# A two-layer mixture-of-experts kernel: sums of x in one piece, branch hints one instruction block ahead, layer 0's branch behind its fourth pair

## Chip, cores, metric

The kernel runs on one core of one Trainium2 chip. The metric is the time of one execution on the device in microseconds (us); less is better. Its engines are TensorE (PE, matrix products), VectorE (DVE), ScalarE (ACT), GpSimd (POOL) and SyncE (SP, which here issues most of the DMAs and does no arithmetic). Each engine works through its own list of instructions in order; semaphores make one wait for another.

## What is computed

Sixteen batches of 256 rows by 256 columns go through two residual layers. Which weights a batch meets depends on its row of `cond_8`.

```python
expert = jnp.argmax(opcode_onehot, axis=-1)                     # layer 0: one of 8 experts
up   = einsum('bsd,bhd->bsh', x, W_up[expert]) + b_up[expert]
gate = einsum('bsd,bhd->bsh', x, W_gate[expert]) + b_gate[expert]
x = x + einsum('bsh,bdh->bsd', silu(up) * gate, W_down[expert]) + b_down[expert]

rw = softmax(cond); w, sel = top_k(rw, 2); w = w / w.sum()      # layer 1: two of 8 experts
mlp(x, g, u, d) = (gelu(x @ g) * (x @ u)) @ d
x = x + sum_k w_k * mlp(x, expert sel_k) + mlp(x, shared)
```

The hidden width is 512 in layer 0 and 1024 in layer 1. All is float32.

## The kernel before

**Units.** Two batches that use the same expert make a Pair; a batch left over is a Single. A Pair's products are done with seven matrix products of half-size blocks where eight would be needed by the plain rule: `STEPS` lists them, with the blocks of the weights (A11, S2, ...) and of x (B11, T2, ...). The blocks named S and T are sums and differences, and have to be made first:

- of x: `sums_x` (L455) with `sums_b` (L467 to L473), three DVE operations, one of 512 columns (L470) and two of 256 (L471, L472). They write `bt` (layer 0) or `xt` (layer 1), and in layer 0 the second writes a `dz` buffer.
- of the up and gate weights of one quarter: `sums_q` (L483), four POOL operations (L478 to L481), or for the shared expert a DMA of sums kept in DRAM.
- of the down weights: `sums_d` (L500), the same four on larger blocks.
- of the activations, before the down product: `act_sums` (L584), again `sums_b`.

**Quarters.** A Pair's hidden width is cut in `kp` parts, two in layer 0 and four in layer 1, each called a quarter here. `up(j, k)` (L536) issues product k of quarter j into a PSUM bank: X, Y and Q, two banks each. After product 0, 2 and 4 ACT copies X out (`copy`, L525); DVE adds or subtracts that copy and Y or Q into `c` (`combine`, L529), which is what lets the bank be used again. `act` (L569) has ACT apply gelu (L573) or silu (L580) and DVE multiply by the gate (L574, L581). `down(k)` (L589) issues the down products into banks A, B (one each) and Y; `early` reads bank A (in layer 1 on ACT, L621; in layer 0 on DVE, L616), and `late` writes the result `ys` (L628, L632).

**Order.** Everything is written out by hand by `Line` (L820). It keeps a clock in which each of the first six products of a quarter counts 2. `main` issues a product, moves the clock and then issues whatever `later` has due. Instructions due at the same time go in the order of their due times. So the order on every engine follows from the due times: product 6 of a quarter is due 4 after its other products, its `act` 6, its `act_sums` 12, the down products 18 and on after the Pair's last quarter.

When a quarter begins, `quarter` (L879) calls `ahead` (L845), which issues the loads: q (up and gate weights) five quarters ahead, sums_q and x three ahead, the sums of x one ahead (L862 to L865), and the quarter's own down weights d. `when_free` puts a step off until a buffer is given back. `quarter` then sends results of earlier units, and runs `route` (L910): the sorting of batches by expert for layer 1 is recorded as a list of small DVE steps, and one to a few are issued per quarter.

**The work and its two branches.** How many Pairs and Singles there are depends on the data. Layer 0 always has batch 0 alone (`l0_first`), one more Single and four Pairs (`l0_pairs`); its remainder is zero to three Pairs and Singles. Layer 1 has eight Pairs on the shared expert (`shared`), twelve Pairs for certain (`pairs`), and zero to four more. A program is written out for each count, and every engine jumps to the one it needs with a table branch: `arms(0)` after `units[0]`, and inside each arm `arms(1)`. In this run both remainders are three Pairs. The register that chooses is loaded in `announce` (L893), which also gives each engine a hint of where its branch (line L1077) will lead. Before the change `units[0]` are the first two Pairs of layer 0, `tails[0]` the other two, and all five engines are hinted at the same point: when the last-but-one quarter of the last unit before the branch begins (L887 to L889). Behind the first branch come the two Pairs of `tails[0]`, then the first five shared Pairs with layer 0's remainder between them, then layer 1's Pairs.

Of the kernel before, what the change touches and what calls it, by code (L numbers as in the profile page):

```python
# [11 lines left out]
ALU = mybir.AluOpType  # L12
# [8 lines left out]
NPR = B // 2  # L21
NA = 2 * B

NP1 = (B - 1 - E + 1) // 2
NP2 = (NA - E) // 2
NS1, NS2 = B - 1 - 2 * NP1, NA - 2 * NP2
NF = 5
NB = 3
# [23 lines left out]
C11, C21, C12, C22 = range(4)  # L52
# [7 lines left out]
def kernel(  # L60
# [8 lines left out]
    out: bass.AP,  # L69
):  # L70
    nc = tc.nc
    SP, POOL = mybir.EngineType.SP, mybir.EngineType.Pool
    ENGINES = [SP, POOL, *(getattr(mybir.EngineType, e) for e in ("PE", "DVE", "Activation"))]
    ctx.enter_context(tc.manual_schedule())

    const = ctx.enter_context(tc.tile_pool(name="const", bufs=1))
# [98 lines left out]
    made = {}  # L175
    steps = [[]]

    class Recorder:
# [5 lines left out]
        @staticmethod  # L184
        def step():
            steps.append([])
# [27 lines left out]
    def order_of_work(v, n, at, layer):  # L214

        tt, red = v.tensor_tensor, v.tensor_reduce
        a, b = square(0, n), square(1, n)  # L220
        numn = num[:, :n]

        def rows(t):
            return t.unsqueeze(2).to_broadcast([P, n, n])

        def cols(t):
            return t.unsqueeze(1).to_broadcast([P, n, n])

        def small(name, dt=F32):
            return const.tile([P, n], dt, name=f"{name}_{layer}")  # L230

        count, rank, odd, key, pos = map(small, ("count", "rank", "odd", "key", "pos"))
        ri = small("ri", I32)
        tt(b, rows(numn), cols(numn), ALU.is_gt)
        step(v)
        tt(a, rows(at), cols(at), ALU.is_equal)
        step(v)
        red(count, a, AX.X, ALU.add)
        step(v)
        tt(a, a, b, ALU.mult)  # L240
        step(v)
        red(rank, a, AX.X, ALU.add)
        step(v)

        v.tensor_copy(ri, rank)
        v.tensor_single_scalar(ri, ri, 1, ALU.bitwise_and)
        v.tensor_copy(odd, ri)
        tt(count, count, rank, ALU.subtract)
        tt(count, count, odd, ALU.add)
        v.tensor_scalar(count, count, 1.0, 4096.0, ALU.is_equal, ALU.mult)  # L250
        v.scalar_tensor_tensor(key, at, float(n), numn, ALU.mult, ALU.add)
        tt(key, key, count, ALU.add)
        tt(a, rows(key), cols(key), ALU.is_gt)
        step(v)
        red(pos, a, AX.X, ALU.add)
        step(v)
        tt(a, rows(numn), cols(pos), ALU.is_equal)
        step(v)

        def sorted_(dst, x):  # L260
            tt(b, a, x, ALU.mult)
            step(v)
            red(dst, b, AX.X, ALU.add)
            step(v)

        t = small("t")
        sorted_(t, cols(at))
        as_index(v, exs[layer], t, E, E - 1)
        made[layer, "e"] = len(steps)
        i = num[:, :B].unsqueeze(1).unsqueeze(1).to_broadcast([P, n, n // B, B])  # L270
        a4, b4 = (q.rearrange("p s (k b) -> p s k b", b=B) for q in (a, b))
        tt(b4, a4, i, ALU.mult)
        step(v)
        red(t, b, AX.X, ALU.add)
        step(v)
        as_index(v, bs[layer], t, 0, B - 1)
        made[layer, "b"] = len(steps)

        red(more, count, AX.X, ALU.add)
        step(v)  # L280
        v.tensor_scalar(more, more, -1.0 / (2 * 4096), E / 2, ALU.mult, ALU.add)
        v.tensor_scalar(more_i[layer], more, 0.0, float(MOST[layer]), ALU.max, ALU.min)
        if layer:
            sorted_(wsort, cols(wts.rearrange("p k b -> p (k b)")))
            v.tensor_scalar(nwsort, wsort, -1.0, None, ALU.mult)
# [7 lines left out]
    more = const.tile([P, 1], F32, name="more")  # L293
    MOST = ((NS1 - 1) // 2, NS2 // 2)
    more_i = [const.tile([P, 1], I32, name=f"more_{i}") for i in range(2)]
# [154 lines left out]
    class Pair(Unit):  # L450
        width, last = 2, False
        first, step = 18, None


        def sums_x(self, spread):  # L455

            self.x = {n: self.xt[:, i, :] for n, i in B_AT.items()}
            if not self.layer:
                self.x["T2"] = take("dz", S, of=(self, "T2"))
            for i, f in enumerate(self.sums_b(self.xt, self.x["T2"])):  # L460
                if spread:
                    line.later(2 + 4 * i, f)
                else:
                    f()

        @staticmethod
        def sums_b(t, t2):  # L467
            tt = nc.vector.tensor_tensor
            return (
                lambda: tt(t[:, 4:6, :], t[:, 0:3:2, :], t[:, 2:4, :], ALU.subtract),  # L470
                lambda: tt(t2, t[:, C22, :], t[:, 4, :], ALU.add),  # L471
                lambda: tt(t[:, 6, :], t[:, C21, :], t2, ALU.subtract),  # L472
            )  # L473

        @staticmethod
        def sums_a(a, s):
# [35 lines left out]
        def load_z(self):  # L512

            self.z = take("z", KD, 2, S)
            self.stores = [], []
            self.out = [self.row(out, t, e) for t, e in enumerate((SP, mybir.EngineType.Activation))]
            for t in range(2):
                nc.sync.dma_start(self.z[:, :, t, :], self.row(out, t))

# [63 lines left out]

        def act_sums(self, j):  # L584
            t = self.acts[j]
            for f in self.sums_b(t, t[:, 2, :]):
                f()

        def down(self, k):  # L589

# [189 lines left out]
    l0_first = First(next(names), 0, B - 1)  # L780
    l0_one = Single(next(names), 0, B - 2)
    l0_pairs = [Pair(next(names), 0, 2 * i) for i in range(NP1)]
    l0_more = [Pair(next(names), 0, 2 * NP1 + 2 * i) for i in range(MOST[0])]
    l0_ones = [Single(next(names), 0, 2 * NP1 + i) for i in range(NS1 - 1)]
    l0_one.po_bank = "A"
    shared = [Pair(next(names), 1, None, (2 * i, 2 * i + 1)) for i in range(NPR)]
    pairs = [Pair(next(names), 1, 2 * i) for i in range(NP2)]
# [2 lines left out]
    shared[-1].last = True  # L790
    shared[-2].step = 7

    units = [l0_pairs[: NP1 - 2], [*pairs, *shared[NF : NPR - NB]]]
    tails = [l0_pairs[NP1 - 2 :], shared[-NB : 1 - NB]]

    among = {
        u: [[] for _ in range(u.kp)] for u in [*l0_pairs, *l0_more, *pairs, *more_pairs, *shared]
# [22 lines left out]
    class Line:  # L820
# [24 lines left out]
        def ahead(self, i):  # L845

            at = dict(enumerate(quarters))
            if i + Q_AHEAD in at:
                u, j = at[i + Q_AHEAD]
                u.load_q(j)  # L850
            if i + S_AHEAD in at:
                u, j = at[i + S_AHEAD]
                if u.width == 2:
                    when_free("s", lambda u=u, j=j: u.sums_q(j))
                if j == 0:
                    if u.width == 2 and not u.layer:
                        when_free("bt", u.load_x)
                    else:
                        if u.layer:
                            self.send(0)  # L860
                        u.load_x()
            if i + 1 in at:  # L862
                u, j = at[i + 1]
                if u.width == 2 and j == 0:
                    u.sums_x(i > 1 and at[i][0].width == 2)  # L865
            if i < 0:
                return
            u, j = at[i]
            pair0 = u.width == 2 and not u.layer
            if j == pair0 and u is not l0_first:  # L870
                when_free(u.d_from, u.load_d)
            if pair0 and j:
                self.later(12, u.sums_d)
            elif u.width == 2 and j == 2:
                u.sums_d()
            if u is shared[-1] and j == 2:
                u.load_z()

        def quarter(self, unit, j):  # L879

            self.at += 1
            assert quarters[self.at] == (unit, j)
            self.ahead(self.at)
            self.send()
            for layer in range(2):

                u = units[layer][-1]  # L887
                if (unit, j) == (u, u.kp - 2):
                    self.announce(layer)  # L889
            for _ in range(self.routes(unit, j)):  # L890
                self.route()

        def announce(self, layer):  # L893

            n = MOST[layer] + 1
            self.arm = nc.values_load(
                more_i[layer][0:1, 0:1],
                min_val=0,
                max_val=n - 1,
                skip_runtime_bounds_check_because="held between 0 and the largest",  # L900
            )
            self.hint = tc.switch_hint(dict.fromkeys(ENGINES, self.arm), n)

        def routes(self, unit, j):

# [18 lines left out]
    line = Line()  # L924
# [63 lines left out]
    run(units[0])  # L988
    for k in arms(0):

        mid, further = [*tails[0]], l0_more[:k]
        for i, u in enumerate(shared[:NF]):
            mid.append(u)
            if i < len(further):
# [2 lines left out]
        places = [a for u in mid for a in among[u]]  # L997
        for a in places:
            a.clear()
        pieces = [p for u in l0_ones[2 * k :] for p in (u.ups, u.downs)]  # L1000
        for a, p in zip(places[3:], pieces):
            a.append(p)
        follow([*mid, *units[1], *tails[1]], behind=False)
        run([*mid, *units[1]])
# [77 lines left out]
```

## Time and profile before

| | us |
|---|---|
| time, three runs: median (lowest, highest) | 1071.49 (1070.37, 1071.58) |
| the profiled execution: its time | 1071.98 |
| the profiled execution: its span | 1070.3 |
| TensorE busy | 1043.4 |
| VectorE busy | 784.6 |
| GpSimd busy | 449.7 |
| ScalarE busy | 353.2 |

A span runs from the first instruction of the program to the last; the 1.7 us between span and time lie around it. A matmul's end is modelled, so a busy PE need not be PE at its best, but with one start each 216 ns (the median) the 4750 matmuls alone come to 1026 us. Rows of the profile name the engine, the line of the kernel, the operation, and what it writes and reads (`c<-cp,Q`). In the view of waits a row says who waited for whom: total us, how many times, the longest. In a listing by time a row has start and length in us, and in brackets how long the engine was idle before it and what ended that. "issue" is a wait for nothing that the profile shows, such as the instructions themselves.

### The profile page before, as it was taken

To read this page: it belongs to the slowest core of one execution; us is meant where nothing else is said; L and a number is where in the kernel's file an instruction comes from. 1 tells how busy PE (TensorE), PEld (TensorE's weight loads), DVE (VectorE), ACT (ScalarE), POOL (GpSimd) and SP (SyncE) were. 2 spreads that over 40 slices of the span, in tenths; PEclk is the share of its full clock that TensorE was granted. 3 is DMA by queue.
4 is the path that set the end of the run, shared out by engine and by line. 5 is a ranking of instruction groups with operands and counts; after the bars stand their busy time and mean duration, and the time that the engine had idled before them with its cause. 6 is when DMAs were issued, how large, how long until landed. Compare 5 with 4: busy or idle time off the path is not lost.

```text
span 1070.3 us, 14116 instructions
## 1 busy us (share of the span) xinstructions
PE 1043.4 (97%) x4750; PEld 899.6 (84%) x4750; DVE 784.6 (73%) x1221; ACT 353.2 (33%) x555; POOL 449.7 (42%) x506
## 2 busy tenths in 40 slices
PE   9989999999999999999999999999999999999997
PEld 6777888888878888888888888888888888888886
DVE  7789988878787777787778777777765335776664
ACT  2332343434333333333333333333323123333331
POOL 2837432221033764566476457546201245620000
PEclk9999999999999999999999999999999999999999
DMA  6636666656673355335334524533735545355532
GB/s 250 225 108 210 213 201 175 219 159 235 197 248 103 87 135 138 98 99 138 92 89 135 137 90 107 138 89 89 198 93 189 174 128 155 91 177 170 186 77 44
DMA packets 58963, 157.52 MB, mean 147 GB/s; under 512 B 5490, under 2 KB 25074, under 8 KB 54642
## 3 DMA queue, kind: packets, MB, share of 16 engines
q1 hardware_dynamic: 45602, 140.90, 39.3%
q0 software_dynamic: 12976, 15.21, 9.6%
q8 instruction: 43, 0.70, 0.3%
q14 instruction: 54, 0.44, 0.1%
q10 hardware_dynamic: 288, 0.26, 0.1%
HBM read 132.23 MB, written 24.12 MB: 146 GB/s over the span
## 4 chain that ended last, share of the span: by engine, by line
PE 80%; DVE 12%; ACT 3%; issue 3%; POOL 0%; DMA 0%; SPq 0%; DVEq 0%; ACTq 0%; POOLq 0%
PE X L544 20%; PE Q L544 14%; PE Y L544 14%; PE A L599 11%; PE B L599 8%; PE Y L599 5%; DVE c L529 5%; DVE bt L574 3%; ACT c L573 2%; PE X L692 2%; PE Q L692 2%; DVE bt L470 1%; DVE xt L471 1%; PE A L722 1%; ACT dz L621 1%
## 5 line engine op out<-in xcount | busy, mean ns | idle before, releaser
L525 ACT ACTIVATE cp<-X 128x512 f32<-128x512 f32 x318 | 189.1, 596 | 540.1 <-PE X L544 539.9
L544 PE MATMUL Y<-xt,q 128*128 128x256 f32 x736 | 192.7, 384 | 11.5 <-DVE c L529 8.9
L574 DVE TENSOR_TENSOR bt<-c 128x1024 f32<-128x1024 f32 x92 | 128.7, 1399 | 94.4 <-ACT c L573 94.4
L544 PE MATMUL Q<-xt,s 128*128 128x256 f32 x736 | 189.6, 380 | 2.5 <-DVE c L529 2.5
L544 PE MATMUL X<-xt,s 128*128 128x256 f32 x736 | 189.5, 380 | 0.0
L544 PEld LDWEIGHTS Y<-xt,q 128*128 128x128 f32 x736 | 137.9, 191 | 39.8 <-DVE c L529 19.4
L529 DVE TENSOR_TENSOR c<-cp,Q 128x512 f32<-128x512 f32 x212 | 144.2, 680 | 32.4 <-ACT cp L525 28.2
L544 PEld LDWEIGHTS Q<-xt,s 128*128 128x128 f32 x736 | 139.3, 190 | 23.6 <-DVE c L529 4.9
L443 POOL DMA_DIRECT2D out_dram<-ys x46 | 49.0, 1066 | 258.1 <-DVE ys L628 102.7
L544 PEld LDWEIGHTS X<-xt,s 128*128 128x128 f32 x736 | 139.3, 190 | 20.5 <-ACT cp L525 1.4
L529 DVE TENSOR_TENSOR c<-cp,Y 128x512 f32<-128x512 f32 x212 | 144.0, 679 | 15.2 <-PE Y L544 10.2
L478 POOL TENSOR_TENSOR s<-q 128x256 f32<-128x256 f32 x78 | 70.2, 900 | 125.0 <-PE Q L544 61.9
L481 POOL TENSOR_TENSOR s<-s,q 128x256 f32<-128x256 f32 x78 | 63.6, 815 | 106.1 <-PE Q L544 102.8
L573 ACT ACTIVATE c<-c 128x1024 f32<-128x1024 f32 x92 | 96.8, 1052 | 20.8 <-DVE c L529 20.8
L599 PE MATMUL B<-bt,ds 128*128 128x256 f32 x424 | 102.2, 381 | 0.0
L470 DVE TENSOR_TENSOR bt<-bt 128x512 f32<-128x512 f32 x113 | 101.3, 897 | 0.3 <-DMA bt<-x_dram 0.2
L599 PE MATMUL A<-bt,ds 128*128 128x256 f32 x424 | 101.3, 379 | 0.0
L544 PE MATMUL X<-xt,q 128*128 128x256 f32 x368 | 94.4, 379 | 0.0
L599 PEld LDWEIGHTS B<-bt,ds 128*128 128x128 f32 x424 | 81.0, 191 | 11.6 <-ACT ys L737 0.3
L599 PE MATMUL Y<-bt,d 128*128 128x256 f32 x376 | 90.0, 379 | 0.0
L599 PEld LDWEIGHTS A<-bt,ds 128*128 128x128 f32 x424 | 80.6, 190 | 11.0
L479 POOL TENSOR_TENSOR s<-s,q 128x256 f32<-128x256 f32 x78 | 78.0, 1000 | 7.1 <-PE A L722 1.1
(165 smaller groups left out, 1161.1 us busy)
## 6 DMA issues: line engine op xcount, KB each, us to landing
q<-wq_dram SPq DMA_DIRECT2D x100, 512.0 KB, 3.6
d<-wd_dram SPq DMA_DIRECT2D x22, 1024.0 KB, 6.6
s<-qsums SPq DMA_DIRECT2D x28, 512.0 KB, 4.7
xt<-x1d SPq DMA_DIRECT2D x46, 256.0 KB, 4.6
out_dram<-ys POOLq DMA_DIRECT2D x46, 256.0 KB, 5.7
q<-wq_dram SPq DMA_DIRECT2D x16, 514.0 KB, 4.6
ds<-dsums SPq DMA_DIRECT2D x7, 1024.0 KB, 6.1
d<-wd_dram SPq DMA_DIRECT2D x7, 513.0 KB, 5.8
```

The lines of the kernel that those rows point to most:

```text
L443: nc.gpsimd.dma_start(row(out), ys[:, :, t, :], accum_op=ALU.add)
L470: lambda: tt(t[:, 4:6, :], t[:, 0:3:2, :], t[:, 2:4, :], ALU.subtract),
L478: tt(s("S1"), a("A21"), a("A22"), ALU.add)
L479: tt(s("S2"), s("S1"), a("A11"), ALU.subtract)
L481: tt(s("nS4"), s("S2"), a("A12"), ALU.subtract)
L525: nc.scalar.activation(t, self.banks["X", j], AF.Copy)
L529: nc.vector.tensor_tensor(self.c[j][:, block].rearrange("p m s -> p (m s)"), self.copies[n, j], self.banks[tag, j], op,)
L544: nc.tensor.matmul(self.banks[tag, j][:, bass.ts(m, S)], lhsT=self.q[j][:, m, A_AT[a], :] if a in A_AT else self.s[j][:, m, S_AT[a], :], r ...
L573: nc.scalar.activation(u, u, AF.Gelu_apprx_tanh)
L574: nc.vector.tensor_tensor(t[:, 0:4, :], u, v, ALU.mult)
L599: nc.tensor.matmul(d, lhsT=src[:, j, :], rhs=self.acts[j][:, B_AT[b], :], start=OPENS[k] and j == 0, stop=j == self.kp - 1, skip_group_che ...
L692: nc.tensor.matmul(dst[:, bass.ts(half, S)], lhsT=self.q[j][:, m, 2 * half + c, :], rhs=self.xt[:, c, :], start=(c == 0), stop=(c == KD - 1),)
```

## The change

Three edits:

1. `sums_x` issues its three DVE operations together. Before, where the quarter in front belongs to a Pair too, they were due 2, 6 and 10 after that quarter's start; now all three are due at 5. (Where it doesn't, they are issued at once, as before.)
2. Hints are given by engine, at places listed in `announces`. For the first branch SP, POOL, ACT and DVE are hinted as the first quarter of layer 0's first Pair begins, PE as the last quarter of its third begins. For the second branch SP is hinted six Pairs before the end of `pairs`, POOL and ACT four, DVE three (its second quarter) and PE in the last Pair (its second quarter). The steps that make layer 1's count end in a step of their own, so that the steps recorded behind them (the sorting of the weights) move one quarter later.
3. `units[0]` are all four Pairs of layer 0, and the first branch comes behind the fourth. `tails[0]` is the first shared Pair, which is now used only to know the quarters that follow. Singles of layer 0's remainder would be placed four quarters in, not three. With this, a Pair of layer 0 asks for its d at its first quarter, not at its second (`j == 0` for `j == pair0`), or as soon as a buffer for it is given back.

```diff
@@ order_of_work @@
         v.tensor_scalar(more_i[layer], more, 0.0, float(MOST[layer]), ALU.max, ALU.min)
+        step(v)
+        made[layer, "more"] = len(steps)
         if layer:
@@ Pair @@
-        def sums_x(self, spread):
-
+        def sums_x(self):
             self.x = {n: self.xt[:, i, :] for n, i in B_AT.items()}
             if not self.layer:
                 self.x["T2"] = take("dz", S, of=(self, "T2"))
-            for i, f in enumerate(self.sums_b(self.xt, self.x["T2"])):
-                if spread:
-                    line.later(2 + 4 * i, f)
-                else:
-                    f()
+            self.sums_b(self.xt, self.x["T2"])
@@ units and hints @@
-    units = [l0_pairs[: NP1 - 2], [*pairs, *shared[NF : NPR - NB]]]
-    tails = [l0_pairs[NP1 - 2 :], shared[-NB : 1 - NB]]
+    units = [l0_pairs, [*pairs, *shared[NF : NPR - NB]]]
+    tails = [shared[:1], shared[-NB : 1 - NB]]
+    announces = [
+        [(l0_pairs[0], 0, [SP, POOL, ACT, DVE]), (l0_pairs[2], 1, [PE])],
+        [
+            (pairs[-6], 0, [SP]),
+            (pairs[-4], 0, [POOL, ACT]),
+            (pairs[-3], 1, [DVE]),
+            (pairs[-1], 1, [PE]),
+        ],
+    ]
@@ Line.ahead @@
                 if u.width == 2 and j == 0:
-                    u.sums_x(i > 1 and at[i][0].width == 2)
+                    self.later(5 if i > 1 and at[i][0].width == 2 else 0, u.sums_x)
+                    self.flush(self.clock)
...
-            if j == pair0 and u is not l0_first:
+            if j == 0 and u is not l0_first:
                 when_free(u.d_from, u.load_d)
@@ Line.quarter @@
             for layer in range(2):
-                u = units[layer][-1]
-                if (unit, j) == (u, u.kp - 2):
-                    self.announce(layer)
+                for i, (*at, engines) in enumerate(announces[layer]):
+                    if [unit, j] == at:
+                        self.announce(layer, engines, i == 0)
@@ Line.announce @@
-        def announce(self, layer):
+        def announce(self, layer, engines, first):
             n = MOST[layer] + 1
-            self.arm = nc.values_load(
+            if first:
+                self.arm = nc.values_load(
...
-            self.hint = tc.switch_hint(dict.fromkeys(ENGINES, self.arm), n)
+            hint = tc.switch_hint(dict.fromkeys(engines, self.arm), n, None if first else self.hint)
+            self.hint = hint
@@ behind the first branch @@
-        mid, further = [*tails[0]], l0_more[:k]
+        mid, further = [], l0_more[:k]
...
-        for a, p in zip(places[3:], pieces):
+        for a, p in zip(places[4:], pieces):
             a.append(p)
```

`sums_b` now issues its three operations itself rather than returning them, for x and for the activations alike.

More of the change, by code (lines that the diff above doesn't have):

```diff
@@ L71 @@
     nc = tc.nc
-    SP, POOL = mybir.EngineType.SP, mybir.EngineType.Pool
-    ENGINES = [SP, POOL, *(getattr(mybir.EngineType, e) for e in ("PE", "DVE", "Activation"))]
+    SP, POOL, PE, DVE, ACT = (
+        getattr(mybir.EngineType, e) for e in ("SP", "Pool", "PE", "DVE", "Activation")
+    )
     ctx.enter_context(tc.manual_schedule())
@@ L468, in sums_b @@
             tt = nc.vector.tensor_tensor
[L469 to L473, printed above, removed]
+            tt(t[:, 4:6, :], t[:, 0:3:2, :], t[:, 2:4, :], ALU.subtract)
+            tt(t2, t[:, C22, :], t[:, 4, :], ALU.add)
+            tt(t[:, 6, :], t[:, C21, :], t2, ALU.subtract)
         @staticmethod
@@ L515, in load_z @@
             self.stores = [], []
-            self.out = [self.row(out, t, e) for t, e in enumerate((SP, mybir.EngineType.Activation))]
+            self.out = [self.row(out, t, e) for t, e in enumerate((SP, ACT))]
             for t in range(2):
@@ L585, in act_sums @@
             t = self.acts[j]
-            for f in self.sums_b(t, t[:, 2, :]):
-                f()
+            self.sums_b(t, t[:, 2, :])
         def down(self, k):
@@ L885, in quarter @@
             for layer in range(2):
-                u = units[layer][-1]
-                if (unit, j) == (u, u.kp - 2):
-                    self.announce(layer)
+                for i, (*at, engines) in enumerate(announces[layer]):
+                    if [unit, j] == at:
+                        self.announce(layer, engines, i == 0)
             for _ in range(self.routes(unit, j)):
                 self.route()
-        def announce(self, layer):
+        def announce(self, layer, engines, first):
             n = MOST[layer] + 1
-            self.arm = nc.values_load(
[L897 to L901, printed above, removed]
-            self.hint = tc.switch_hint(dict.fromkeys(ENGINES, self.arm), n)
+            assert not layer or self.routed >= made[1, "more"]
+            if first:
+                self.arm = nc.values_load(
+                    more_i[layer][0:1, 0:1],
+                    min_val=0,
+                    max_val=n - 1,
+                    skip_runtime_bounds_check_because="held between 0 and the largest",
+                )
+            hint = tc.switch_hint(dict.fromkeys(engines, self.arm), n, None if first else self.hint)
+            self.hint = hint
         def routes(self, unit, j):
```

## The prediction

> **What bounds the kernel now.** First the page: busy shares, then the chain of work that ended last.
>
> ```profile
> PE 1043.4 (97%) x4750; PEld 899.6 (84%) x4750; DVE 784.6 (73%) x1221; ACT 353.2 (33%) x555; POOL 449.7 (42%) x506
> PE 80%; DVE 12%; ACT 3%; issue 3%; POOL 0%; DMA 0%; SPq 0%; DVEq 0%; ACTq 0%; POOLq 0%
> ```
>
> TensorE (PE) has work for all but about 27 us of the 1070.3 us span, so an edit that leaves its matmuls alone can win only what PE waits. Hence the view of waits, for PE alone:
>
> ```profile
> PE Y L544 <- DVE c L529: 8.9, 15, 0.8
> PE Q L544 <- DVE c L529: 2.9, 3, 1.8
> PE X L544 <- issue: 2.8, 1, 2.8
> PE Y L544 <- DVE ys L632: 2.2, 1, 2.2
> PE Q L544 <- POOL s L481: 1.9, 1, 1.9
> ```
>
> Three places. Nine of the fifteen waits of the first row are 0.83 to 0.85 us long and come once per layer 1 pair from 412 to 713 us. The 1.8 us of the second row is at 797 us, behind the second branch. The other three rows, with 0.4 us more at 43.5 us, are the first 102 us: layer 0's pairs and the first branch. For the first place I read VectorE (DVE) in order of time over one pair's end, PE's wait being at 487.88 to 488.72:
>
> ```profile
> 478.63 0.68 DVE L470 TENSOR_TENSOR xt<-xt 128x512 f32<-128x512 f32 x1
> 479.36 0.69 DVE L529 TENSOR_TENSOR c<-cp,Y 128x512 f32<-128x512 f32 x1
> 480.15 0.69 DVE L529 TENSOR_TENSOR c<-cp,Q 128x512 f32<-128x512 f32 x1
> 483.25 0.48 DVE L628 SCALAR_TENSOR_TENSOR ys<-B,nwsort,dz 128x256 f32<-128x256 f32 x1 [2.41 <-ACT dz L621]
> 484.56 1.71 DVE L574 TENSOR_TENSOR bt<-c 128x1024 f32<-128x1024 f32 x1 [0.83 <-ACT c L573]
> 486.19 0.94 DVE L471 TENSOR_TENSOR xt<-xt 128x256 f32<-128x256 f32 x1
> 487.06 0.68 DVE L529 TENSOR_TENSOR c<-cp,Q 128x512 f32<-128x512 f32 x1
> 487.66 0.41 DVE L472 TENSOR_TENSOR xt<-xt 128x256 f32<-128x256 f32 x1
> 487.99 0.68 DVE L529 TENSOR_TENSOR c<-cp,Y 128x512 f32<-128x512 f32 x1
> ```
>
> DVE stands idle for 2.41 us, then does two of the next pair's sums (xt, L471 and L472) between operations that PE waits for: the last row empties the Y bank. For the other places, DVE at the second branch, then busy time by stretch (columns: length, PE, PEld, DVE, ACT, POOL, PE clock, DMA share, GB/s):
>
> ```profile
> 789.59 0.42 DVE L472 TENSOR_TENSOR bt<-bt 128x256 f32<-128x256 f32 x1
> 794.47 0.06 DVE L393 MEMSET q<- 1x1 f32 x1 [4.46 <-issue]
> ```
> ```profile
> 36.00:102.00 66.00, 58.66 (x268) 49.82 (x266) 57.70 (x91) 21.57 (x36) 40.76 (x52) 1.00 0.52 172
> 102.00:110.00 8.00, 8.00 (x30) 6.81 (x31) 7.93 (x13) 1.77 (x3) 6.62 (x10) 0.80 0.24 96
> ```
>
> At 789.82 DVE branches and its next instruction comes at 794.26. In layer 0 PE and DVE are both needed for some 58 of 66 us: whichever is freed soon meets the other.
>
> [...]all five engines stand at both branches (PE 3.56 and 1.8 us, DVE 2.8 and 4.4, ScalarE 2.7 and 2.5, GpSimd 2.5 and 2.6, SyncE 4.7 and 3.6), though each had a hint. [...]PE's instruction queue moved 16 KB a packet (0.70 MB in 43) and the other 8 KB (0.44 MB in 54)[...]. [...]L471 on xt takes 417 ns at the least and 942 in the median. [...] After the 2.25 us gap at 99.67 eight matmuls took 3.62 us in the chain where 1.73 is usual (clock 0.80 above); after the longer gap at 59.45 none did. So I price it at 1.9 us, as chance.
>
> **The change, step by step.** Taking the path that this run took (three pairs of the remainder in each layer), the changed program has on every engine the same instructions as before, and PE's matmuls in the same order. Only places move.
>
> Sums of x. All three now stand right behind c<-cp,Q of 480.15, ahead of L628. Alone they take 0.68 + 0.42 + 0.41 = 1.5 us, beside GpSimd (rows of 1.40, 0.83 and 0.83 at 468.9) 3.1. From 480.84 this ends at 482.4 or 483.9. L628 (0.48) must be done by 484.56, where L574 is released by ScalarE: it is, in both. Cover: the 2.41 and 0.83 us of idleness. Behind L574 the two c then run at 486.2 and 486.8, and Y is free at 487.5 instead of 488.67; PE wants it at 487.88. Saved 9 x 0.84 = 7.5 us; bounds 0 (something else is late by as much) and 7.9 (with two waits of 0.17). What is late next has 0.4 us to spare. x was asked for at 459 and takes 4.8 us in the median to land, so the sums' own wait is none. The waits of 0.7 and 0.3 at 309 and 319 have the same cause, with recorded steps of the order of work near (moved one quarter later, 1.2 us each): I take 0.8 of 1.4, with the 0.35 at 768; bounds 0 and 1.4.
>
> Second branch. When is a hint of use? [...] PE's hint in front of the second branch was 185 instructions early[...]: its packet came at 783.19, before the branch at 783.72, and it stood 1.8 us rather than 3.56. DVE's hint was 30 early[...], and helped nothing. [...] DVE's 4.4 us go, and with them PE's 1.78. PE's own stall there was covered by its queue, the others by loads 5 quarters ahead: 0. Total 1.8; bounds 0 and 1.8.
>
> First branch and layer 0. [...] SyncE: d of the first two pairs is now asked for sooner (behind q at 30.14 and at 41.93, not at 35.12 and 44.96), so GpSimd need not idle 3.4 us for it at 37.6, and the 1.9 us wait for s goes; for later pairs d stands ahead of q and the x1d stores, waiting for PE's last down matmul (about 0.9 us at 71), against 5 quarters of q in hand. d of the third pair lands near 77 instead of 84.09, which thins GpSimd's unbroken run from 84 to 108 beside DVE. But PE cannot take 7.3 us: DVE is as full. Its idle 8.3 us are 2.84 of branch, 3.6 before L581, 0.9 for bank A, the rest small. Filling L581's waits with the sums yields about 2, the moved branch 2.84, less its new place (about 106 us, where DVE has no slack): 0.3 or 2.8, so 1.5 at even odds. That is 3.3, and half of the 1.9 of clock: 4.2. Bounds: -1 (branch missed, sums in the way) and 9.2 (all of 7.3 + 1.9).
>
> Sum: 7.5 + 0.8 + 1.8 + 4.2 = 14.3. The profiled execution took 1071.98 (span 1070.3 and 1.7 around it), giving 1057.7; the median 1071.49 is 0.5 below it, so 1057.2 to 1057.7. I take 1057.5.
>
> **Rivals.** A: layer 0 stays bound by DVE, so freed PE waits there come back as waits for c or ys. For: 57.7 of 66 us busy, and PE's restart at 62.27 found its Y bank emptied only at 62.15. Against: 2.84 us of branch idleness. 7.5 + 0.8 + 1.8: 1061.5. B: the sums win nothing, since GpSimd slows them and c is late anyway. For: L574 takes 1.71 beside GpSimd where 1.23 is usual. Against: even at 3.1 us they fit. 0.8 + 1.8 + 4.2: 1064.8. A hint that does nothing costs 1.8 more in either. C, slower: in layer 0 the sums stand ahead of dz (L616), which empties the only A bank; dz ended at 97.40 and PE used A at 97.78. It is so between layer 0's pairs 1 to 3 and behind the last: three times. Moved by 1.21 + 0.94 + 0.84 = 3.0 us, less 0.4 of slack, and with 1.9 of half clock each, that costs 3 x 4.5 = 13.5 against the 10.1 won elsewhere: 1075. It decides from 3.4 us a time on. Against: the first sum leaves the place ahead of c, so dz moves by less.
>
> **Numbers.** Measurement tells about 0.2% (2 us). Forecast 0.60; A 0.20; B 0.12; C 0.06; within 0.2% 0.02. Faster 0.92. The range runs from all of layer 0 won (7.5 + 0.8 + 1.8 + 9.2 = 19.3: 1052.5) to past B, 1066.
>
> **What would show it.** Right: no wait of 0.84 us for c in 412 to 713; the sums directly behind c<-cp,Q inside the idle 2.4 us; DVE's gap at the second branch under 1 us; the wait for s gone. Wrong: waits of PE on L529, or on ys and dz, in the first 110 us that add up to 7 again; new gaps of PE in 110 to 300, where it has none now.

## The result, and the profile after

The changed kernel took 1053.13 us in the median of four runs (1052.21 to 1053.54); the kernel before took 1070.93 beside it (1069.47 to 1071.58). The ratio is 0.9834, with a 95% interval from 0.9817 to 0.9851. The profiled execution took 1053.26 us, its span 1051.6. Both runs took three pairs of the remainder in each layer, with the same 4750 matmuls, so the start of one and the same matmul can be compared in the two traces.

| matmuls that start in (us of the kernel before) | gained there, us | what lies there |
|---|---|---|
| 0 to 118 | 3.4 | layer 0, first branch |
| 118 to 300 | 0 | first shared pairs |
| 300 to 377 | 1.9 | short waits for c |
| 377 to 716 | 9.85 | nine layer 1 pairs |
| 716 to 790 | 0.8 | short waits for c |
| 790 to 805 | 2.05 | second branch |
| to the end | 0.2 | |

The span's other 0.5 us lie behind the last matmul.

Read the page of the changed kernel in the same order as before. First the busy shares, then the chain:

```profile
PE 1038.3 (99%) x4750; PEld 899.9 (86%) x4750; DVE 783.0 (74%) x1221; ACT 353.6 (34%) x555; POOL 446.9 (42%) x506
PE 88%; DVE 8%; issue 2%; ACT 1%; POOL 1%; DMA 0%; SPq 0%; DVEq 0%; ACTq 0%; POOLq 0%
```

The chain now runs through PE for 88% of the span, not 80%. DVE does the same work (783 us) but lies on the chain for 8%, not 12%. The waits of PE in the changed kernel (total us, times, longest):

```profile
PE A L594 <- DVE dz L611: 1.6, 2, 1.1
...
PE Q L540 <- POOL ds L477: 1.1, 1, 1.1
PE Q L540 <- POOL bq L493: 1.1, 1, 1.1
PE Y L540 <- DVE ys L627: 0.9, 2, 0.7
PE Q L540 <- DVE c L525: 0.7, 1, 0.7
...
PE Y L540 <- DVE c L525: 0.4, 2, 0.2
```

The row of 8.9 us for c has shrunk to two waits of 0.2, and the 2.8 us of "issue" are gone. What is left is nearly all in layer 0; the wait of 0.7 for c is at 306 us. The same pair's end on DVE as was shown before, now (start, length, idle before):

```profile
472.59 0.69 DVE L525 TENSOR_TENSOR c<-cp,Q 128x512 f32<-128x512 f32 x1
473.19 0.78 DVE L467 TENSOR_TENSOR xt<-xt 128x512 f32<-128x512 f32 x1
474.01 0.42 DVE L468 TENSOR_TENSOR xt<-xt 128x256 f32<-128x256 f32 x1
474.47 0.43 DVE L469 TENSOR_TENSOR xt<-xt 128x256 f32<-128x256 f32 x1
475.69 0.48 DVE L623 SCALAR_TENSOR_TENSOR ys<-B,nwsort,dz 128x256 f32<-128x256 f32 x1 [0.79 <-ACT dz L616]
476.99 1.71 DVE L570 TENSOR_TENSOR bt<-c 128x1024 f32<-128x1024 f32 x1 [0.82 <-ACT c L569]
478.63 0.67 DVE L525 TENSOR_TENSOR c<-cp,Q 128x512 f32<-128x512 f32 x1
479.22 0.68 DVE L525 TENSOR_TENSOR c<-cp,Y 128x512 f32<-128x512 f32 x1
```

The three sums take 1.7 us of the 2.4 that DVE waited for dz; 0.79 us are left. Behind L570 nothing stands ahead of the two c, and Y is emptied 2.9 us after L570 began, where it was 4.1. By the starts of its matmuls each of the nine waits of 0.84 us was worth 1.11 (nine of them 10.0; other small waits take back 0.15). Why it is more than the wait itself shows in the chain of the kernel before, behind one of these waits (start, length, what):

```profile
488.72 1.13 PE Y L544 x4
489.85 0.86 PE Q L544 x4
```

The first four matmuls after the wait take 1.13 us, the next four the usual 0.86: a restart costs 0.27. Of this, 0.10 is the second matmul, which starts 0.32 us behind the first and not 0.22; the rest is the part of a matmul's modelled 0.38 us that the next one otherwise overlaps. Busy time hides both, since they count as busy. Counting matmuls does not. Here is the stretch of 412 to 714 us, the kernel before and then the changed one (length, then busy time and number of PE, PEld, DVE, ACT, POOL, PE clock, DMA share, GB/s):

```profile
412.00:714.00 302.00, 294.45 (x1346) 254.12 (x1344) 231.97 (x315) 102.15 (x161) 181.47 (x176) 1.00 0.42 113
```
```profile
412.00:714.00 302.00, 301.54 (x1391) 263.32 (x1390) 236.93 (x322) 105.67 (x166) 186.93 (x183) 1.00 0.43 117
```

PE gains 7.1 us of busy time there, but 45 matmuls, which is 9.7 us at one each 216 ns. DVE at the second branch of the changed kernel:

```profile
773.26 0.42 DVE L469 TENSOR_TENSOR bt<-bt 128x256 f32<-128x256 f32 x1
774.25 0.06 DVE L396 MEMSET q<- 1x1 f32 x1 [0.56 <-issue]
```

0.56 us stand where there were 4.46. By the records of the branch instructions all five engines pass this branch in 0.3 to 0.5 us. At the first, PE passes in 0.34, ScalarE in 0.4 and DVE in 0.6; SyncE still stands 2.9 us and GpSimd about 3.5, and no PE wait follows from those. Layer 0 by stretch in the changed kernel, the columns as above:

```profile
36.00:102.00 66.00, 61.29 (x278) 51.65 (x276) 60.16 (x96) 21.55 (x36) 42.23 (x54) 1.00 0.49 162
102.00:110.00 8.00, 7.90 (x37) 6.64 (x36) 7.49 (x12) 2.88 (x5) 6.92 (x9) 1.00 0.51 178
```

PE does 10 matmuls more in the first stretch and 7 more in the second, whose clock is no longer halved (1.00, where it was 0.80).

### The profile page after: what moved, and what is told of

The parts are those of the page before. It is cut to its first block, busy times and chain, and to the rows that moved or that the text cites. A ratio compares the mean times of both kernels' runs of the same rounds, so it can differ in the third digit from the quotient of the medians.

```text
span 1051.6 us, 14115 instructions
## 1 busy us (share of the span) xinstructions
PE 1038.3 (99%) x4750; PEld 899.9 (86%) x4750; DVE 783.0 (74%) x1221; ACT 353.6 (34%) x555; POOL 446.9 (42%) x506
## 4 chain that ended last, share of the span: by engine, by line
PE 88%; DVE 8%; issue 2%; ACT 1%; POOL 1%; DMA 0%; SPq 0%; DVEq 0%; ACTq 0%; POOLq 0%
PE X L540 23%; PE Q L540 16%; PE Y L540 16%; PE A L594 12%; PE B L594 9%; PE Y L594 8%; DVE c L525 3%; PE X L687 2%; PE Q L687 1%; DVE bt L467 1%; PE A L717 1%; PE B L717 1%; DVE bt L577 1%; DVE bt L570 1%; DVE bt L468 1%
## 5 line engine op out<-in xcount | busy, mean ns | idle before, releaser
L570 DVE TENSOR_TENSOR bt<-c 128x1024 f32<-128x1024 f32 x92 | 128.9, 1401 | 90.8 <-ACT c L569 90.8
L540 PE MATMUL Y<-xt,q 128*128 128x256 f32 x736 | 190.3, 381 | 0.8 <-DVE c L525 0.4
```

What stands on the lines that cost most here:

```text
L540: nc.tensor.matmul(self.banks[tag, j][:, bass.ts(m, S)], lhsT=self.q[j][:, m, A_AT[a], :] if a in A_AT else self.s[j][:, m, S_AT[a], :], r ...
L570: nc.vector.tensor_tensor(t[:, 0:4, :], u, v, ALU.mult)
```

## Experiments

The theory: the time lay in where the sums of x stand on DVE, which delays the c that empties Y; the branches add their own stops; layer 0 wins little, being as full on DVE as on PE. Every time below is a median of four to six runs, beside the kernel before on the same chip.

**The first edit alone, and all but the first edit.** `sums_alone` is the kernel before with the three sums issued together at 5; `sums_apart` is the changed kernel with this undone.

```diff
-            for i, f in enumerate(self.sums_b(self.xt, self.x["T2"])):
-                if spread:
-                    line.later(2 + 4 * i, f)
...
+                    self.later(5 if i > 1 and at[i][0].width == 2 else 0, u.sums_x)
```

> The kernel before with the first edit alone (the three sums of x together, due 5). By theory, the nine waits of 0.84 us in layer 1 and their restart (each is followed by four matmuls that take 1.13 us, not 0.86) go, and so do the smaller waits from 305 to 376 us: 9.9 + 1.5 = 11.4 us, 1059.5. Rival: the sums give only what the waits themselves add up to in the view of waits, 7.5 + 0.8: 1062.6. Second rival: the sums win in layer 1 and lose in layer 0, where they stand ahead of dz: 1061 to 1063 with PE waiting for dz before 102 us.

Measured: 1060.02 us beside 1070.21, ratio 0.9901 (0.9886 to 0.9916). So the edit is worth 10.2 us by itself, near the theory's 11.4. But the starts of the matmuls split this into two parts: from 118 us to the second branch it gains 12.8, while layer 0 loses 2.7. PE's gap at the first branch, which stays where it was, is 4.0 us, not the 2.8 us of before, and the clock behind it falls (0.63 over 62 to 70 us); the fallen clock alone makes 2.7 us there. The first row is from the view of waits of `sums_alone`, the second its stretch of 62 to 70 us (in the kernel before the clock was 1.00 there, with 36 matmuls):

```profile
PE X L540 <- issue: 4.0, 1, 4.0
```
```profile
62.00:70.00 8.00, 7.61 (x23) 6.30 (x24) 2.84 (x4) 0.84 (x2) 1.96 (x4) 0.63 0.01 4
```

> The changed kernel (1053.1 us) with the first edit undone: the three sums of x are due 2, 6 and 10 after the quarter's start again; hints and layer 0's branch stay as changed. The complement of sums_alone (1060.0, which is 10.2 under the kernel before at 1070.2). Theory (the parts don't add: the sums worsen layer 0 while its branch stands behind the second pair, so layer 0's part is worth 7 beside them but only the 3.4 that the two traces show without them, and the second hints 2): 1070.2 - 3.4 - 2.0 = 1064.8. Rival (layer 0's part is worth 7 in either case): 1070.2 - 7 - 2 = 1061.2. Rival (the parts add): 1053.1 + 10.2 = 1063.3.

Measured: 1065.84 us beside 1071.24, ratio 0.9954 (0.9941 to 0.9968). That is nearest to the first theory (1064.8); the rivals had 1061.2 and 1063.3, and the second of these is not far outside the interval. Without the sums' edit, hints and moved branch are worth 5.4 us. The nine waits are back, in its view of waits:

```profile
PE Y L546 <- DVE c L531: 8.0, 12, 0.9
```

Undoing the sums' edit in the changed kernel costs 12.7 us by the medians and 10.7 by the two spans; alone the edit won 10.2 and 10.8. So for the whole kernel it is not shown that the sums win more beside the other edits. In layer 0 it shows, as a table below tells.

**The sums in one piece, at another place.**

```diff
-                    self.later(5 if i > 1 and at[i][0].width == 2 else 0, u.sums_x)
+                    self.later(7 if i > 1 and at[i][0].width == 2 else 0, u.sums_x)
```

> The changed kernel (1053.1 us) with its three sums of x still issued together, but two units of the clock later (due at 7, not 5): on VectorE they then stand behind the product L574 instead of ahead of ys, between it and the two c that empty Q and Y. Theory (what pays is the place, inside VectorE's 2.4 us of idleness): now all 1.5 us of the sums (2.3 beside GpSimd) stand ahead of the two c, where the kernel before had 1.35 us of them, so each of the nine layer 1 pairs in 412 to 713 us has a wait of PE of 0.9 to 1.8 us for c again, with 0.27 us of restart each: 1053 + 9 x (1.2 to 2.1) = 1064 to 1072. Rival (what pays is that they are in one piece): no wait comes back, 1053 to 1054.

Measured: 1090.05 us beside 1070.47, ratio 1.0176 (1.0153 to 1.0199). The place decides, not the one piece. DVE at a pair's end in this kernel:

```profile
494.17 1.71 DVE L570 TENSOR_TENSOR bt<-c 128x1024 f32<-128x1024 f32 x1 [0.82 <-ACT c L569]
495.80 1.21 DVE L467 TENSOR_TENSOR xt<-xt 128x512 f32<-128x512 f32 x1
497.05 0.42 DVE L468 TENSOR_TENSOR xt<-xt 128x256 f32<-128x256 f32 x1
497.50 0.42 DVE L469 TENSOR_TENSOR xt<-xt 128x256 f32<-128x256 f32 x1
497.85 0.68 DVE L525 TENSOR_TENSOR c<-cp,Q 128x512 f32<-128x512 f32 x1
498.44 0.68 DVE L525 TENSOR_TENSOR c<-cp,Y 128x512 f32<-128x512 f32 x1
```

All three sums stand ahead of both c, and PE waits 1.7 us here. The expected 1064 to 1072 was too low, because it counted the nine pairs alone. By the starts of the matmuls their stretch (377 to 716 us) accounts for 16.7 us of the loss, inside the expected 11 to 19. The other 20 us come from the other pairs, in layer 0 with a lower clock too: 0.95 in the mean of 36 to 102 us, where the kernel before had 1.00. PE's waits in all:

```profile
PE Y L540 <- DVE c L525: 22.1, 17, 1.7
PE Q L540 <- DVE c L525: 6.4, 6, 2.6
PE Y L540 <- DVE ys L627: 5.4, 5, 2.3
```

**The second branch's hints at the old point.**

```diff
-            (pairs[-6], 0, [SP]),
-            (pairs[-4], 0, [POOL, ACT]),
-            (pairs[-3], 1, [DVE]),
-            (pairs[-1], 1, [PE]),
+            (pairs[-1], 2, [SP, POOL, PE, DVE, ACT]),
```

> The changed kernel with the second branch's hints where they were: all five engines in the last Pair's third quarter. By theory VectorE stands 2.5 to 4.5 us at the branch again and PE then waits 1.8 to 2.0 us for c: 1055.2 against 1053.1. Rival: PE's own stall of 1.8 us counts on top now that it has no other waits, 1057. Second rival: the waits are hidden now, since VectorE is ahead: 1053.1.

Measured: 1054.48 us beside 1070.21, ratio 0.9847 (0.9834 to 0.9861): 1.3 us above the changed kernel's median, 1.2 where the traces part at the branch. PE itself passes in 0.31 us here (1.8 in the kernel before), so its hint served at the old point this time. DVE stands its four microseconds again:

```profile
773.20 0.43 DVE L469 TENSOR_TENSOR bt<-bt 128x256 f32<-128x256 f32 x1
777.64 0.06 DVE L396 MEMSET q<- 1x1 f32 x1 [4.02 <-issue]
```

But PE's wait behind it is 0.9 us, not 1.8. `sums_alone`, with the same sums and the old hints, tells why:

| | DVE's branch ahead of the start of PE's wait | DVE's stop | PE's wait |
|---|---|---|---|
| before | 7.24 | 4.44 | 1.78 |
| `sums_alone` | 7.65 | 4.51 | 1.44 |
| `second_hints_old` | 7.65 | 4.00 | 0.93 |

Beside the new sums DVE is 0.4 us further ahead, which shortens the wait by as much. The rest is DVE's own stop, which differed by 0.5 us between two kernels with the same sums and the same hint point. With the restart, the hints are worth 2.05 us beside the sums' old places and 1.2 to 1.7 beside their new ones.

**Layer 0's part undone, the rest as changed.**

```diff
-    units = [l0_pairs, [*pairs, *shared[NF : NPR - NB]]]
-    tails = [shared[:1], shared[-NB : 1 - NB]]
+    units = [l0_pairs[: NP1 - 2], [*pairs, *shared[NF : NPR - NB]]]
+    tails = [l0_pairs[NP1 - 2 :], shared[-NB : 1 - NB]]
...
-        [(l0_pairs[0], 0, [SP, POOL, ACT, DVE]), (l0_pairs[2], 1, [PE])],
+        [(l0_pairs[1], 0, [SP, POOL, PE, DVE, ACT])],
...
-            if j == 0 and u is not l0_first:
+            if j == pair0 and u is not l0_first:
...
```

> The changed kernel with all of layer 0 as before: branch behind the second Pair, its five hints at one point, d asked for at the second quarter; sums of x and second hints stay changed. By theory layer 0's part of the change was 3.4 to 3.7 us (1.5 to 1.9 of it the half clock behind 99.67 us): 1056.7. Rival: the sums alone already took the half clock away, and the branch's place is worth under 1 us: 1054. Second rival: the branch stall of PE comes in full, 2.8 us, with the half clock: 1058.

Measured: 1060.09 us beside 1070.21, ratio 0.9897 (0.9882 to 0.9912), 7 us above the changed kernel. All three expectations were too low. The trace: PE's stop at the branch is back, the clock behind it is 0.59 (64 to 70 us), and 1.8 us of wait for dz follow at 102.

```profile
PE X L540 <- issue: 3.6, 2, 3.3
PE A L594 <- DVE dz L611: 3.2, 2, 1.8
```

With `sums_apart` this gives layer 0 in all four combinations (us gained over the kernel before, in the matmuls up to its 118 us):

| | layer 0 as before | layer 0 as changed |
|---|---|---|
| sums as before | 0 | 3.4 (`sums_apart`) |
| sums together | -2.7 (`sums_alone`), -4.0 (`layer0_old`) | 3.4 (changed kernel) |

So layer 0's part is worth 3.4 us beside the old sums and 6.2 to 7.4 beside the new ones. The loss of the two kernels with the new sums and the old branch lies around that branch (4.1 and 4.5 us in the matmuls of 56 to 75 us): the lower clock, 2.7 us in `sums_alone`, and a longer gap (4.0 and 3.3 us, where it was 2.8). That the sums lengthen the stop is not shown: PE's branch instruction took 3.56 us in the kernel before, 4.53 in `sums_alone` and 3.67 in `layer0_old`. Why the clock fell there, and not behind the gap of the kernel before, is not shown.

**Which piece of layer 0's part.** Five kernels. First, `layer0_old` with PE's hint a pair earlier:

```diff
-        [(l0_pairs[1], 0, [SP, POOL, PE, DVE, ACT])],
+        [(l0_pairs[0], 0, [PE]), (l0_pairs[1], 0, [SP, POOL, DVE, ACT])],
```

> layer0_old (1060.1 us: the changed sums and second hints, layer 0's branch behind its second pair with the old hint point and d at the second quarter) with one thing changed: TensorE's hint for the first branch is given at the first quarter of layer 0's first pair[...]; the other four engines keep the old point. Theory (the 7 us that layer 0's part is worth beside the sums are TensorE's own 3.3 us at the branch and the half clock of 2.3 us behind it, not the branch's new place): PE's gap at 60.7 us falls under 1 us and the clock stays whole, 1060.1 - 5.6 = 1054.5, at the most back to 1053. Rival (VectorE's own stop at the same branch, 2.8 us at 65 us, takes its place as a wait of PE for c, so moving the branch is what paid): at the most 2 us won, 1058 to 1060.

Measured: 1058.01 us beside 1070.47, ratio 0.9878 (0.9859 to 0.9898). The number is the rival's, but it does not speak for the rival, since the edit did not do what it was made for: PE stops at the branch all the same.

```profile
PE X L540 <- issue: 4.0, 1, 4.0
```

The hint ran at 24.1 us, the next packet of the 16 KB instruction queue came at 31.2, the branch at 57.9. I had expected the hint to serve; it did not, and I don't know why. So the two hints of the first branch were tried in the changed kernel itself, each moved close to the branch:

```diff
-        [(l0_pairs[0], 0, [SP, POOL, ACT, DVE]), (l0_pairs[2], 1, [PE])],
+        [(l0_pairs[0], 0, [SP, POOL, ACT, DVE]), (l0_pairs[3], 1, [PE])],
...
+                        late = 8 if not layer and i else 0
+                        self.later(late, partial(self.announce, layer, engines, i == 0))
...
```

> The changed kernel (1053.1 us) with TensorE's hint for the first branch 35 instructions ahead of it instead of 264[...] (it is due 8 units of the clock behind the start of the fourth pair's last quarter). Theory (the hint saves TensorE's own stop at the branch): a gap of 2.8 to 4 us marked issue at 97 us, with 2.3 us of half clock behind it if the clock falls: 1056 to 1059. Rival (VectorE, which runs some 4 us behind at this branch, is what counts there; layer0_old_early_pe_hint pointed that way): 1053 to 1054.5.

Measured: 1055.11 us beside 1071.24, ratio 0.9854 (0.9838 to 0.987). PE stops, as the theory said, but for less, and the clock stays whole (1.00 in the mean of the execution):

```profile
PE X L540 <- issue: 1.8, 1, 1.8
```

PE's hint is worth 2.0 us at this place (the wait of 1.8 and its restart).

```diff
-        [(l0_pairs[0], 0, [SP, POOL, ACT, DVE]), (l0_pairs[2], 1, [PE])],
+        [(l0_pairs[0], 0, [SP, POOL, ACT]), (l0_pairs[2], 1, [PE]), (l0_pairs[3], 1, [DVE])],
```

> The changed kernel (1053.1 us) with VectorE's hint for the first branch at the fourth pair's last quarter, 26 instructions ahead of the branch instead of 127. Theory (it misses, and VectorE, as full as TensorE there, hands its stop on): VectorE stands 2.8 to 4.4 us at 102 us instead of 0.6, and PE waits 1.5 to 3.5 us for c or ys near 107 us: 1055 to 1057. Rival (the stop is covered, since the shared pair that follows leaves VectorE time): 1053 to 1053.5.

Measured: 1054.99 us beside 1071.24, ratio 0.9851 (0.9838 to 0.9863). DVE stands 3.08 us, with nothing to cover it:

```profile
102.05 0.42 DVE L469 TENSOR_TENSOR bt<-bt 128x256 f32<-128x256 f32 x1
105.56 1.23 DVE L924 TENSOR_TENSOR ys<-num 128x1024 f32<-128x1024 f32 x1 [3.08 <-issue]
```

Of the 2.6 us by which the stop is longer than with the hint that served, 1.8 reach PE as waits for c and ys from 106.9 us on, with their restarts; the time rises by 1.9. The question how early a hint may be:

```diff
-        [(l0_pairs[0], 0, [SP, POOL, ACT, DVE]), (l0_pairs[2], 1, [PE])],
+        [(l0_pairs[0], 0, [SP, POOL, ACT, DVE, PE])],
```

> The changed kernel (1053.1 us) with TensorE's hint for the first branch given with the others at the first quarter of layer 0's first pair: 640 instructions ahead of the branch[...]. In layer0_old_early_pe_hint a hint 291 ahead[...] did not spare the stop (4.5 us). Theory 1 ([...]that failure had another cause): PE passes the branch in 0.3 us, 1053.1. Theory 2 ([...]an early one is lost): a gap marked issue of 2.8 to 4.5 us at 97 us, 1056 to 1059.

Measured: 1052.33 us beside 1071.24, ratio 0.9827 (0.9813 to 0.9841): PE passes in 0.34 us. The hint 640 instructions ahead served as well as the one 264 ahead, so earliness alone is not what failed in `layer0_old_early_pe_hint`, where it was 291 ahead.

The last edit of layer 0's part is d at a pair's first quarter. Undone:

```diff
-            if j == 0 and u is not l0_first:
+            if j == pair0 and u is not l0_first:
```

> The changed kernel with a layer 0 Pair's d asked for at its second quarter again. Theory of the prediction: GpSimd then waits for d, s comes late and PE waits about 1 us more at 43 to 52 us: 1054. Rival, from the trace after: what PE waits for there is VectorE's c (it ends at 44.44 and 52.05, PE starts at 44.58 and 52.15), GpSimd is not the cause, and d's place is worth 0.3 us or less: 1053.1.

Measured: 1053.21 us beside 1070.21, ratio 0.9841 (0.9827 to 0.9854): no difference that the interval shows. It lies nearest to the rival's number (1053.1), and the trace goes against the theory: PE's wait at 43.5 us does not grow but goes, and so do those for dz; one of 1.2 us put down to s stays, and longer waits for ys come.

**Room left in layer 0.** In the changed kernel the sums stand ahead of dz, as the prediction's rival C described. DVE there:

```profile
56.13 1.08 DVE L467 TENSOR_TENSOR bt<-bt 128x512 f32<-128x512 f32 x1
57.25 0.83 DVE L468 TENSOR_TENSOR dz<-bt 128x256 f32<-128x256 f32 x1
58.12 0.84 DVE L469 TENSOR_TENSOR bt<-bt,dz 128x256 f32<-128x256 f32 x1
58.88 0.47 DVE L611 SCALAR_TENSOR_TENSOR dz<-A,d,bt 128x256 f32<-128x256 f32 x1
```

PE waits 1.07 us for this dz. The edit puts dz first; `dz_ahead_and_d_late` adds the later d.

```diff
-                line.later(self.first + step * k, lambda k=k: self.down(k))
+                line.later(self.first + step * k - (k == 0 and not self.layer), lambda k=k: self.down(k))
```

> The changed kernel (1053.1 us) with layer 0's first down product of each pair due one unit of the clock earlier, so that on VectorE dz (L616, which empties bank A) stands ahead of the next pair's sums of x. PE's two waits for dz (1.07 and 0.57 us, at 58.4 and 78.3) are to go. Theory (layer 0 is bound by VectorE as much as by TensorE): they come back as waits for ys or c, 1052.8 to 1053.5. Rival (the order dz behind sums costs what it shows, as rival C of the prediction had it): 1.6 us less, 1051.5.

> The kernel of dz_ahead_of_sums with layer 0's d asked for at a pair's second quarter as in the kernel before. Theory (VectorE bounds layer 0, neither edit lowers its load): 1052.5 to 1053.5, no difference that can be measured. Rival (the two are worth something together, since d at the second quarter removed PE's wait at 43.5 us and showed 2.4 us less in its one profile): 1050.5 to 1051.5.

Measured: 1053.30 us, ratio 0.984 (0.9818 to 0.9863), and 1051.72, ratio 0.9823 (0.9805 to 0.984), both beside 1070.47. The waits for dz are gone and others stand in their place; here is the row of `dz_ahead_of_sums`, then that of `d_at_second_quarter`, where the two dz waits had also gone:

```profile
PE Y L540 <- DVE ys L627: 3.1, 3, 1.6
```
```profile
PE Y L540 <- DVE ys L627: 3.5, 4, 1.5
```

Layer 0 keeps its time with dz first: the matmul that starts at 118 us in the kernel before starts at 114.68 us in `dz_ahead_of_sums` and at 114.67 in the changed kernel. The second kernel has the lowest median of all, but its interval covers the changed kernel's ratio: no gain is shown.

## Why the prediction was right, and where its terms were off

It gave 1057.5 by a sum of 14.3 us; 17.8 came in the medians, 18.7 in the two spans. The main mechanisms were those it named. The time came near the lower end of its range (1052.5), but not for the reason given there, all of layer 0 won: layer 0 gave 3.4 of 9.2 us, and restarts and small waits made up the rest. By its steps:

- **Sums of x, 7.5.** The place was right to a few tenths: the sums follow c<-cp,Q, Y is free before PE asks, and no wait of 0.84 us is left from 412 to 713. Mis-sized: the stretch gave 9.85 (the other traces with the sums together, and in the place of the change, gave 9.8 to 11.5). The step priced the wait and left out the restart, 9 x 0.27 = 2.4.
- **Small waits, 0.8 of 1.4.** 1.9 came from 300 to 377 us and 0.8 from 716 to 790, so 2.7. Of the three waits listed, those of 0.32 and 0.35 are gone. The largest, 0.73 at 309, is not: it stands at 306 in the changed kernel, as 0.68, so "the same cause" was wrong for it. What came instead were waits of under 0.2 us in other pairs, each worth its restart too.
- **Second branch, 1.8.** 2.05 between the two traces, restart included. This holds beside the old sums; beside the new ones, hinting at the old point costs 1.2 (`second_hints_old`) or 1.7 (`sums_alone`).
- **First branch and layer 0, 4.2.** 3.4 between the traces. PE passed in 0.34 us; of the "even odds" for the moved branch the better came, DVE passing in 0.6; GpSimd and SyncE stood 3.5 and 2.9 us. "DVE is as full" fits the two dz kernels, whose freed waits came back as others. The half clock at 102 us is gone (1.00 over 102 to 110 us, where it was 0.80), priced at half of 1.9 as chance; no gap of PE in the changed kernel's layer 0 exceeds 1.1 us.
- **The wait for s.** This step failed: "GpSimd need not idle 3.4 us, and the 1.9 us wait for s goes". PE still waits 1.07 us at 51.1, and asking for d earlier or later changes the time by nothing that can be measured. In the kernel before, PE restarted at 52.31, DVE's c<-cp,Q having ended at 52.21; in the changed kernel it restarts at 52.15, c having ended at 52.05. In all thirteen traces that have this wait PE restarts 0.10 us after that c ended. GpSimd's last operation mostly ended within 0.02 us of c, so the row could name it; but the operation named differs (of s, ds or bq), and in `layer0_old` it had ended 0.65 us before. So PE waited for c, which empties the bank.
- **Rival C.** Its mechanism is there: 1.07 and 0.57 us for dz, where it priced 4.5 each. It cost nothing in the end, since the dz kernels show the next wait close behind.
- **The sum.** Adding the parts fitted the total better than it deserved. The prediction took the terms for independent, and in layer 0 they are not: its part is worth 3.4 us beside the old sums and 6.2 to 7.4 beside the new, whose traces have the longer gap at the first branch (4.0 and 3.3 us) and the lower clock behind it (0.63 over 62 to 70 us, 0.59 over 64 to 70). With the hint and the new place together PE passes in 0.34 us and the clock is 1.00 over 36 to 102 and 102 to 110 us.

Open: what makes a hint serve. That PE's and DVE's would serve at their new places was an estimate, and it came true (0.34 and 0.6 us at the first branch). But the distance to the branch does not tell the cases apart: at the first branch PE's hint served 264 and 640 instructions ahead, and did not 35 ahead (`pe_hint_inside_block`, a gap of 1.8 us) and 291 ahead (`layer0_old_early_pe_hint`, 4.0 us); DVE's served 127 ahead and did not 26 ahead (`dve_hint_inside_block`, 3.08 us idle). At the second branch PE passed in 0.32 us in the changed kernel, but stood 3.6 us in `layer0_old` and 3.4 in `layer0_old_early_pe_hint`, with the same hints. At most 0.28 us of these two stops became a gap. What decides is not shown.

## What to carry over

Read an engine's order around each wait for what stands ahead of the operation that frees a bank, and move independent work into idle time in front of it: the same three operations won 10 us at one place and cost 37 us, against the changed kernel, 2 clock units later. Price each removed wait with its restart (here 0.84 + 0.27), by counting matmuls rather than busy time. Don't add what parts win: make one run without each part, and compare the starts of the same matmuls stage by stage, as the worth of a hint or a branch depended on the other edits.

## What the runs showed of the hardware

- Of a taken branch: where a hint served, PE took 0.34 us at the first branch and 0.32 at the second (changed kernel), and the other engines 0.4 to 0.6. Where it did not, the engines stood 1.8 to 4.7 us (kernel before, both branches). At the first branch PE stood 3.56 us in the kernel before, 3.67 in `layer0_old` and 4.53 in `sums_alone`, and its matmuls had gaps of 2.8, 3.3 and 4.0 us there. At the second branch of the kernel before PE stood 1.8 us, from 783.72 us on, and its matmuls had no gap.
- Of PE's clock behind a gap: the length of the gap alone did not tell. The clock was lower behind gaps of 3.3 us (`layer0_old`, 0.59 over 64 to 70 us) and 4.0 us (`sums_alone`, 0.63 over 62 to 70 us), and also behind 2.25 us (kernel before, 99.67 us). `sums_behind_product`, with gaps of 2.56 and 2.28 us at 43.5 and 81.5 us, had 0.86 over 40 to 52 us and 0.95 over 36 to 102. Behind the 2.8 us at 59.45 us in the kernel before it stayed whole. In the kernel before, behind the gap of 59.45 to 62.27 us, then before and behind that of 99.67 to 101.92 us (columns: length, then busy time and number of PE, PEld, DVE, ACT, POOL, PE clock, DMA share, GB/s):

```profile
62.00:70.00 8.00, 7.74 (x36) 6.86 (x37) 5.09 (x11) 1.69 (x3) 3.08 (x4) 1.00 0.18 71
98.40:101.81 3.41, 1.27 (x6) 0.76 (x5) 3.41 (x6) 1.11 (x3) 3.33 (x4) 1.00 0.74 219
101.81:105.22 3.41, 3.30 (x8) 2.69 (x9) 3.34 (x7) 0.00 (x0) 3.01 (x5) 0.50 0.45 182
```

Eight matmuls fall in the last stretch, at half clock, where 3.41 us hold 15 or 16 at one each 216 ns. Why the clock fell behind the shorter of these two gaps and not behind the longer is not shown.
